# GAT edge values as a row read back from DRAM, and where the softmax of the second layer stands in the round

## The chip, the cores and the metric

The kernel runs on one core of one Trainium2 chip. The core has TensorE for matrix products (PE in the profile; its weight loads are shown as PEld), VectorE (DVE), ScalarE (ACT) and GpSimd (POOL) for everything elementwise, and SyncE (SP), whose queue issues nearly all transfers here. The metric is the time of one execution on the device in microseconds, and the number given is the median of three runs.

## The reference

64 graphs of 256 nodes with 512 features go through two layers. Each layer normalises its input, cuts it at zero, computes a graph operator on it and adds the result to its input.

```
h = max(layernorm(x), 0)
# layer 0: gated attention, 8 heads of 64
q, k, v = h Wq.T, h Wk.T, h Wv.T
c = softmax(q k.T / 8 where adj != 0) v
gate = sigmoid([c, h] Wg.T + bg)
x = x + gate * h + (1 - gate) * c
# layer 1: GAT, one head
h = max(layernorm(x), 0)
Wh = h W
e[i, j] = leaky_relu(Wh[i].a1 + Wh[j].a2, slope 0.2), masked where adj == 0
x = x + elu(softmax(e over j) Wh)
```

All of it is in 32-bit floats. The change concerns layer 1: the values Wh[j].a2 have to stand as a row along the free dimension on all partitions, while the product that makes them leaves them as a column, one value for each node on its partition.

## The kernel before

A graph is two tiles of 128 nodes. The dense products are split into 2 x 2 blocks and done with seven block products in place of eight (Strassen's scheme): `strassen` gives the steps 1 to 7, and the sums between them are named u1, u2, u3 and c00 to c11. u1 and c00 are ACT copies from PSUM, the others are DVE sums of a PSUM bank and an SBUF tile (L185, L187). Three banks a, b and c are shared by all such products; a later step may write into a bank only when the sum that reads it has been done.

The graphs go through a software pipeline. `emit_round(i)` writes out one round by hand, and the order of its calls is the order of instructions on every engine, as the scheduler is told to leave the five engines alone. In round i, graph p = i + 1 is at the q/k and v products, graph i at its attention weights, graph q = i - 1 at the gate, the first residual and the second norm, graph r = i - 2 at Wh, the GAT softmax and its product, and o = i - 3 at the elu, the second residual and the store. On PE a round runs: gate (pma_z to pmc_z), Wh (wh), q/k (qk), v, attention product (pc, L418), scores (ps, L338), GAT product (po, L615).

Transposes over all 128 partitions are mostly done through DRAM: DVE turns 32 x 32 blocks, SP sends the tile to DRAM (`send`, `send_blocks`) and fetches it back with blocks exchanged (`fetch`, `fetch_blocks`). Every such tile is named there_... on its way out: there_e and eT (attention weights; four fetches a round, named by half and pair), there_y and yT (output of the gate), there_h and hT (normalised inputs of both layers), there_g and egT (GAT attention).

SP's queue is in order: a transfer whose semaphores are not there yet holds all that are behind it. The same holds on each engine.

The steps around the change, for graph r, or q where it is said:

- The last column of each half of w1 carries W a1 and W a2, so that Wh holds one more column per half (HH + 1 = 257 columns). The a2 column is `wh[:, t, 1, HH]`.
- `g_edges` (L552 to L556) makes the row of 256 values on all 128 partitions with two PE transposes of the column, broadcast to 128 columns, into a PSUM tile pe.
- `g_logits` (L558 to L564) adds row, own value and mask with one DVE instruction for each of the two tiles; `g_leaky` (L566 to L571) does the leaky relu and the negated maximum; `g_exp` (L578) is ACT; `g_turn_e` (L587 to L598) turns blocks on DVE; `g_send_e` and `g_fetch_e` take the result through DRAM; `g_out` (L611 to L617) needs it as egT.
- For the last three graphs (g >= LAST - 1 = 61) the softmax is transposed on PE in place of DRAM.
- `g_residual` (L502 to L509), for graph q, adds yT to x with one DVE sum per tile; `g_stats` and `g_root` follow.
- `g_elu`, `g_add` (L637, POOL) and `g_store` (L640) end graph o. `load_graph` (L88 to L94) fetches x and adj of graph i + 2 into a pool of five x tiles, so that its x waits for the store of graph o to have landed.
- `a_fetch(i, 1, 1)` is the fourth eT; the second half of pc reads it last.

The pool "tmp" has five buffers of 128 x 512 floats, among them eg and egT; "h" has one, which the normalised inputs and the gate's output y share.

Of the kernel before, what the change touches and what calls it, by code (L numbers as in the profile page):

```python
# [8 lines left out]
F32 = mybir.dt.float32  # L9
# [3 lines left out]
ALU = mybir.AluOpType  # L13
# [9 lines left out]
def kernel(  # L23
# [32 lines left out]
    nc = tc.nc  # L56
    B, N, H = x.shape
    NH = 8
    DK = H // NH
    P = 128  # L60
    HC = H // P
    NT = N // P
    HH = H // 2
    SCALE = 1.0 / DK ** 0.5
    LAST = B - 2
    assert N == 256 and H == 512 and SCALE == 0.125

    def pool(name, bufs, **kw):
        return ctx.enter_context(tc.tile_pool(name=name, bufs=bufs, **kw))
# [3 lines left out]
    sb = {tag: pool(tag, bufs) for tag, bufs in {  # L73
        "x": 5, "adj": 1, "mask": 4, "hT": 3, "S": 3, "qk": 2, "v": 2, "wh": 1, "e": 5,
        "cT": 1, "z": 2, "h": 1, "tmp": 5, "U": 3,
    }.items()}
# [3 lines left out]
    dram = pool("dram", 4, space=bass.MemoryType.DRAM)  # L80
# [6 lines left out]
    graphs = {}  # L87
# [38 lines left out]
    def edge_columns():  # L126

        w = weight["1"]

        def column(c, side):  # L130
            scr = sb["tmp"].tile([P, 2, HH], F32, tag="t", name=f"scr_{c}_{side}")
            nc.vector.scalar_tensor_tensor(
                scr, w[:, c, :, :HH], 1.0, a_sb[side].rearrange("p (n f) -> p n f", n=2),
                ALU.mult, ALU.mult, accum_out=w[:, c, side, HH:],
            )

        return [lambda c=c, side=side: column(c, side) for c in range(HC) for side in range(2)]
# [177 lines left out]
    def on_tokens(w, op):  # L315

        def todo(n):
            return [((), op[n][:, c, :], w[n][:, c, :]) for c in range(2)]
        return todo
# [182 lines left out]
    def g_residual(g, t):  # L502
        s = graphs[g]
        x = s["x"][:, t, :]
        if g >= LAST:
            nc.vector.tensor_tensor(x, x, s["py"][t], ALU.add)
        else:
            x = x.rearrange("p (j i c) -> p j i c", i=4, c=32)
            nc.vector.tensor_tensor(x, x, s["yT"][:, :, t].rearrange("p i j c -> p j i c"), ALU.add)  # L509

    def g_stats(g, t):
        norm_stats(graphs[g], t, f"l1_{g}")
# [33 lines left out]
    def g_wh(g):  # L546
# [2 lines left out]
        dst = [[s["wh"][:, t, n, :] for n in range(2)] for t in range(2)]  # L549
        return strassen(f"wh_{g}", [P, HH + 1], on_tokens(weight["1"], s["h1S"]), dst)  # L550

    def g_edges(g):  # L552
        s = graphs[g]
        pe = s["pe"] = ps["w"].tile([P, N], F32, tag="t", name=f"pe_{g}")
        for t in range(NT):
            nc.tensor.transpose(pe[:, t * P:(t + 1) * P], s["wh"][:, t, 1, HH:].to_broadcast([P, P]), ident)  # L556

    def g_logits(g):  # L558
        s = graphs[g]
        e = s["eg"] = sb["tmp"].tile([P, NT, N], F32, tag="t", name=f"eg_{g}")  # L560
        for t in range(NT):
            nc.vector.scalar_tensor_tensor(
                e[:, t, :], s["pe"], s["wh"][:, t, 0, HH:], s["mask"][:, t, :], ALU.add, ALU.add
            )  # L564

    def g_leaky(g):  # L566
# [79 lines left out]
    def chore(steps, n):  # L646
        for _ in range(min(n, len(steps))):
            steps.pop(0)()

    def emit_round(i):  # L650


        p, q, r, o = i + 1, i - 1, i - 2, i - 3

        def do(fn, g, *args):
            if 0 <= g < B:
                fn(g, *args)

        def run(fn, g, steps):
            if 0 <= g < B:  # L660
                if (fn, g) not in products:
                    products[fn, g] = fn(g), set()
                product, done = products[fn, g]
                for step in steps.split():
                    if step not in done:
                        product(step)
                        done.add(step)
# [52 lines left out]
        do(p_sums, p)  # L720
        do(g_turn, q)
        do(g_send, q)
        do(a_fetch, i, 0, 1)
        run(g_wh, r, "c10 3 c01")
        do(g_fetch, q)
        do(a_fetch, i, 1, 0)

        if i == -1:
            chore(weight_sums("q"), 4)
            chore(weight_sums("k"), 4)  # L730
        run(p_qk, p, "1 u1")
        do(g_edges, r)
        do(g_logits, r)
        do(g_leaky, r)
        run(p_qk, p, "6 u2 5")
        do(g_elu, o, 1)
        do(g_add, o, 1)
        do(g_add, o, 0)
        do(g_store, o)
        do(g_exp, r)  # L740
        do(g_turn_e, r)
        do(g_send_e, r)
        do(g_rec, r)
        run(p_qk, p, "7 u3 c11 2 c00")
        do(load_graph, p + 1)
        if i == -1:
            for key in ("gh", "gc", "1"):
# [3 lines left out]
            chores.append(lambda: nc.vector.tensor_scalar_mul(hbg, hbg, 0.5))  # L751
            chores.extend(edge_columns() + weight_sums("1"))
        chore(chores, 1)
        do(a_fetch, i, 1, 1)
        do(g_fetch_e, r)
        do(g_residual, q, 0)
        run(p_qk, p, "4 c10")
        do(g_residual, q, 1)
        chore(chores, 1)
        run(p_qk, p, "3 c01")  # L760
        chore(chores, 1)
        do(g_stats, q, 0)
        if i == -1:
# [94 lines left out]
```

## Time and profile before

The median of three runs is 3191.97 us (3191.17 to 3193.47). The execution that was profiled took 3185.72 us, 1.8 us more than the span that the profile shows.

| what | value |
|---|---|
| time, median of three | 3191.97 us |
| the profiled execution: time, span | 3185.72 us, 3183.9 us |
| length of a round (1525.81 to 1574.16, pc to pc) | 48.35 us |
| of it busy: PE, DVE, ACT, POOL | 48.35, 38.27, 22.06, 23.52 us |
| share of the DMA engines in that round | 0.80 |
| granted TensorE clock | 0.994 |
| transposes pe on PE (L556) | 128, 274 ns each |
| logits (L562), leaky (L569), maximum (L571) on DVE | 480, 692, 686 ns (middle) |
| first residual on DVE (L509) | 124, 686 ns each |
| second residual on POOL (L637) | 128, 1272 ns each |

Read it in this way. A busy PE is not by itself proof that PE is the limit, so one looks at the chain of waits: the run of work that ended last, followed backwards from the end. Where it stays on one engine without gaps, time falls only if work of that engine falls, and it rises as soon as something else comes too late for it. For an in-order queue the question is which transfer stands behind which wait. Landing times are given from the start of the issue to the last of the data's completion. On the queue, an entry with x4 is four issues in a row.

### The profile page before, as it was taken

How to read it: one execution, taken by the hardware profiler on the slowest of the kernel's cores; microseconds unless marked ns; L12 is line 12 of the kernel's file. 1: busy time of each engine (PE TensorE's matmuls, PEld its weight loads, DVE VectorE, ACT ScalarE, POOL GpSimd, SP SyncE). 2: the span in 40 equal slices, each digit the busy share in tenths (PEclk: the TensorE clock that was granted, in tenths of full speed). 3: DMA queues.
4: the chain of work that ended last, by engine and by line, in shares of the span. 5: the costliest groups of instructions: out<-in, count | busy, mean ns of one | idle time of the engine just before them, and what ended most of it. 6: DMA issues, size and time to landing. Idle time of an engine off the chain costs nothing.

```text
span 3183.9 us, 66670 instructions
## 1 busy us (share of the span) xinstructions
PE 3125.0 (98%) x22716; PEld 2723.9 (86%) x22716; DVE 2467.8 (78%) x6366; ACT 1413.6 (44%) x3976; POOL 1506.3 (47%) x2183
## 2 busy tenths in 40 slices
PE   7899999999999999999999999999999999999997
PEld 6888888888889888888888898888888888888984
DVE  6777877877877878778778778778787787787774
ACT  2343543543544534435435445445344344454442
POOL 2454544544544545535445445445454454454453
PEclk9999999999999999999999999999999999999998
DMA  5678778777777777787787777777877877877761
GB/s 169 176 173 204 189 180 206 185 180 206 182 190 199 184 191 195 180 203 187 178 211 184 181 207 182 190 197 177 200 189 182 205 186 179 211 183 183 204 170 44
DMA packets 1103394, 590.63 MB, mean 186 GB/s; under 512 B 685776, under 2 KB 1029328, under 8 KB 1103056
## 3 DMA queue, kind: packets, MB, share of 16 engines
q1 hardware_dynamic: 1102000, 585.32, 73.9%
q8 instruction: 182, 2.98, 0.4%
q14 instruction: 156, 1.28, 0.1%
q10 hardware_dynamic: 1056, 1.05, 0.1%
HBM read 304.88 MB, written 281.28 MB: 184 GB/s over the span
## 4 chain that ended last, share of the span: by engine, by line
PE 90%; DVE 4%; POOL 2%; DMA 2%; issue 1%; SPq 1%; ACT 0%; DVEq 0%; POOLq 0%; ACTq 0%
PE pmb_qk L174 11%; PE pmb_z L174 9%; PE pc L418 7%; PE pma_qk L174 7%; PE pmc_qk L174 7%; PE ps L338 6%; PE po L615 6%; PE pma_z L174 6%; PE pmc_z L174 6%; PE pmb_v L174 5%; PE pmb_wh L174 5%; PE pma_v L174 3%; PE pmc_v L174 3%; PE pmc_wh L174 3%; PE pma_wh L174 3%; DVE e L353 1%
## 5 line engine op out<-in xcount | busy, mean ns | idle before, releaser
L362 ACT ACTIVATE e<-e,low 128x256 f32<-128x256 f32 x1024 | 506.5, 499 | 63.3 <-DVE low L353 63.3
L204 POOL TENSOR_TENSOR rs_l<-ve_l,mhalf 128x2 f32<-128x2 f32 x128 | 89.0, 695 | 869.7 <-DVE ve_l L200 869.7
L353 DVE CUSTOM_DVE_ANT_0 e<-ps,mask 128x256 f32<-128x256 f32 x1024 | 362.1, 415 | 100.1 <-PE ps L338 100.1
L377 POOL TENSOR_SCALAR e<-e,rec 128x256 f32<-128x256 f32 x768 | 352.7, 477 | 148.8 <-DVE rec L370 100.4
L386 DVE STREAM_TRANSPOSE eb<-e 128x512 f32<-128x512 f32 x512 | 351.8, 696 | 76.7 <-POOL e L377 63.4
L213 ACT ACTIVATE h_l<-x,nb_l,rs_l 128x512 f32<-128x512 f32 x256 | 194.1, 805 | 212.4 <-DVE nb_l L208 123.5
L152 POOL TENSOR_TENSOR S_l<-hT_l 128x256 f32<-128x256 f32 x128 | 93.4, 730 | 395.9 <-DMA hT_l<-there_h 361.9
L637 POOL TENSOR_TENSOR x<-x,pos 128x512 f32<-128x512 f32 x128 | 160.1, 1272 | 229.3 <-DVE pos L633 229.3
L615 PE MATMUL po<-wh,egT 128*128 128x512 f32 x512 | 242.5, 617 | 2.1 <-ACT egT L598 2.1
L338 PE MATMUL ps<-qk 64*128 64x256 f32 x2048 | 238.9, 383 | 0.6 <-DVE v L185 0.6
L418 PE MATMUL pc<-eT,v 128*64 128x256 f32 x2048 | 235.9, 382 | 0.1
L338 PEld LDWEIGHTS ps<-qk 64*128 64x128 f32 x2048 | 193.1, 187 | 45.3 <-DVE ve_l L200 21.9
L418 PEld LDWEIGHTS pc<-eT,v 128*64 128x64 f32 x2048 | 141.3, 137 | 86.7 <-DMA eT<-there_e 16.3
L239 DVE STREAM_TRANSPOSE h_l<-h_l 128x512 f32<-128x512 f32 x248 | 167.8, 695 | 54.7 <-ACT h_l L213 54.7
L615 PEld LDWEIGHTS po<-wh,egT 128*128 128x128 f32 x512 | 94.3, 194 | 118.5 <-issue 95.1
L362 ACT ACTIVATION_READ_ACCUMULATOR e<-e,low 128x1 f32 x1024 | 194.8, 190 | 0.0
L196 DVE BATCH_NORM_STATS2 bs_l<-x 128x6 f32<-128x512 f32 x256 | 172.9, 675 | 5.4 <-DMA x<-in_x_dram 5.4
L461 ACT ACTIVATE z<-z,hbg 128x256 f32<-128x256 f32 x256 | 116.1, 502 | 105.9 <-DVE z L185 105.9
L456 POOL TENSOR_TENSOR d<-hT_l,cT 128x512 f32<-128x512 f32 x128 | 160.5, 1274 | 0.0
L428 ACT COPY cT<-pc 128x512 f32<-128x512 f32 x128 | 74.9, 585 | 184.5 <-PE pc L418 184.5
L174 PEld LDWEIGHTS pma_z<-hT_l,wgh_sb 128*128 128x128 f32 x1024 | 129.2, 192 | 30.4 <-issue 30.4
L174 PE MATMUL pma_qk<-hT_l,wq_sb 128*128 128x128 f32 x1024 | 139.6, 280 | 11.9 <-DMA hT_l<-there_h 10.1
(146 smaller groups left out, 7964.8 us busy)
## 6 DMA issues: line engine op xcount, KB each, us to landing
there_e<-eb SPq DMA_DIRECT2D x256, 512.0 KB, 3.4
eT<-there_e SPq DMA_DIRECT2D x1024, 128.0 KB, 3.9
there_h<-h_l SPq DMA_DIRECT2D x496, 128.0 KB, 3.3
hT_l<-there_h SPq DMA_DIRECT2D x496, 128.0 KB, 3.3
x<-in_x_dram SPq DMA_DIRECT2D x64, 512.0 KB, 4.0
out_dram<-x SPq DMA_DIRECT2D x64, 512.0 KB, 4.2
there_y<-y SPq DMA_DIRECT2D x62, 512.0 KB, 3.3
yT<-there_y SPq DMA_DIRECT2D x248, 128.0 KB, 3.4
```

Of the source, the lines that this page charges most:

```text
L174: nc.tensor.matmul(bank[key][(slice(None), *cols)], lhsT, rhs, start=first and i == 0, stop=last and i == len(todo) - 1, skip_group_check= ...
L196: nc.vector.bn_stats(bs, s["x"][:, t, :])
L213: nc.scalar.activation(h[:, t, :], s["x"][:, t, :], AF.Relu, bias=s["nb"][:, t:t + 1], scale=s["rs"][:, t:t + 1])
L239: nc.vector.transpose(h[:, t, :], h[:, t, :])
L338: nc.tensor.matmul(psc[jj, i][:, t, :], qk[r:r + DK, 0, jj, t * P:(t + 1) * P], qk[r:r + DK, 1, jj, :], start=True, stop=True,)
L353: nc.vector.tensor_tensor_reduce(s["e", half, jj][:, i, t, :], s["ps", half][jj, i][:, t, :], s["mask"][:, t, :], -SCALE, HUGE, ALU.add, A ...
L362: nc.scalar.activation(e, e, AF.Exp, bias=s["low", half][:, jj, i, t:t + 1], scale=-1.0, accum_out=s["sums", half][:, jj, i, t:t + 1],)
L377: nc.gpsimd.tensor_scalar(e, e, rec[:, i, t:t + 1], 1.0, ALU.mult, ALU.mult)
L386: nc.vector.transpose(s["eb", half, jj][:, :, 4 * i:4 * i + 4, :].rearrange("p b n c -> p n b c"), e)
L418: nc.tensor.matmul(pc[i * DK:(i + 1) * DK, jj, :].rearrange("p (t a c) -> p t a c", t=NT, c=32), s["v"][:, kc, hd * DK:(hd + 1) * DK], eT[ ...
L456: nc.gpsimd.tensor_tensor(d, s["hT"][:, :, js, :], s["cT"][:, :, js, :], ALU.subtract)
L615: nc.tensor.matmul(pm, s["egT"][:, t, kc, :], s["wh"][:, kc, :, :HH], start=(kc == 0), stop=(kc == NT - 1))
```

## The change

Three things change.

First, for graphs below 61 the row of a2 values is made without PE. `g_send_edges` writes the column of 256 values from Wh to DRAM (one transfer, elements of four bytes), and `g_fetch_edges` reads those 1,024 bytes back onto each of the 128 partitions, straight into the first half of eg. `g_logits` then reads the row from eg, so it does tile 1 first and tile 0 in place.

Second, the order of the round changes. On SP the two transfers stand around the eT fetch (0, 1), ahead of the yT fetch; the eT fetch (1, 0) goes behind the store; the load of x and adj goes ahead of there_g; the fourth eT fetch stays behind there_g. On DVE the logits, leaky and maximum move from behind the first step of the q/k product to behind u3 and c11; the block transpose of the softmax moves behind c10.

Third, the first residual of graphs below 62 moves from DVE to POOL; its second sum is issued behind the last step of the q/k product.

```diff
             x = x.rearrange("p (j i c) -> p j i c", i=4, c=32)
-            nc.vector.tensor_tensor(x, x, s["yT"][:, :, t].rearrange("p i j c -> p j i c"), ALU.add)
+            nc.gpsimd.tensor_tensor(x, x, s["yT"][:, :, t].rearrange("p i j c -> p j i c"), ALU.add)
...
+    def g_send_edges(g):
+        s = graphs[g]
+        if g < LAST - 1:
+            s["edges"] = dram.tile([NT, P], F32, tag="edges", name=f"edges_{g}")
+            with nc.allow_non_contiguous_dma(reason="a column of 256"):
+                nc.sync.dma_start(s["edges"].rearrange("t p -> p t"), s["wh"][:, :, 1, HH])
+
+    def g_fetch_edges(g):
+        s = graphs[g]
+        if g < LAST - 1:
+            s["eg"] = sb["tmp"].tile([P, NT, N], F32, tag="t", name=f"eg_{g}")
+            row = s.pop("edges").rearrange("t p -> (t p)")
+            nc.sync.dma_start(s["eg"][:, 0, :], bass.AP(tensor=row.tensor, offset=row.offset, ap=[[0, P], [1, N]]))
+
     def g_edges(g):
         s = graphs[g]
+        if g < LAST - 1:
+            return
...
     def g_logits(g):
         s = graphs[g]
-        e = s["eg"] = sb["tmp"].tile([P, NT, N], F32, tag="t", name=f"eg_{g}")
-        for t in range(NT):
+        if g >= LAST - 1:
+            s["eg"] = sb["tmp"].tile([P, NT, N], F32, tag="t", name=f"eg_{g}")
+        e = s["eg"]
+        for t in (1, 0):
             nc.vector.scalar_tensor_tensor(
-                e[:, t, :], s["pe"], s["wh"][:, t, 0, HH:], s["mask"][:, t, :], ALU.add, ALU.add
+                e[:, t, :], s["pe"] if g >= LAST - 1 else e[:, 0, :], s["wh"][:, t, 0, HH:], s["mask"][:, t, :], ALU.add, ALU.add
             )
...
         do(g_send, q)
+        run(g_wh, r, "c10 3 c01")
+        do(g_send_edges, r)
         do(a_fetch, i, 0, 1)
-        run(g_wh, r, "c10 3 c01")
+        do(g_fetch_edges, r)
         do(g_fetch, q)
-        do(a_fetch, i, 1, 0)
...
         run(p_qk, p, "1 u1")
-        do(g_edges, r)
-        do(g_logits, r)
-        do(g_leaky, r)
         run(p_qk, p, "6 u2 5")
         do(g_elu, o, 1)
         do(g_add, o, 1)
         do(g_add, o, 0)
         do(g_store, o)
+        do(a_fetch, i, 1, 0)
+        run(p_qk, p, "7 u3 c11")
+        do(g_edges, r)
+        do(g_logits, r)
+        do(g_leaky, r)
+        run(p_qk, p, "2 c00")
         do(g_exp, r)
-        do(g_turn_e, r)
-        do(g_send_e, r)
-        do(g_rec, r)
-        run(p_qk, p, "7 u3 c11 2 c00")
         do(load_graph, p + 1)
...
+        run(p_qk, p, "4 c10")
+        do(g_turn_e, r)
+        do(g_send_e, r)
         do(a_fetch, i, 1, 1)
+        do(g_rec, r)
+        do(g_residual, q, 0)
         do(g_fetch_e, r)
-        do(g_residual, q, 0)
-        run(p_qk, p, "4 c10")
-        do(g_residual, q, 1)
         chore(chores, 1)
         run(p_qk, p, "3 c01")
+        do(g_residual, q, 1)
```

## The prediction

> **What bounds the kernel now.** I read four views in this order: the page's busy shares and chain, the chain of waits of one round in order of time, the time line of the queues and of VectorE (DVE) and GpSimd (POOL) in that round, and the landing times of single transfers.
>
> ```profile
> PE 3125.0 (98%) x22716; PEld 2723.9 (86%) x22716; DVE 2467.8 (78%) x6366; ACT 1413.6 (44%) x3976; POOL 1506.3 (47%) x2183
> PE 90%; DVE 4%; POOL 2%; DMA 2%; issue 1%; SPq 1%; ACT 0%; DVEq 0%; POOLq 0%; ACTq 0%
> ```
>
> TensorE (PE) is busy for 98% of the span and makes 90% of the chain that ends last; nothing else has 5%. So only two things count: PE work removed, and PE made to wait. One round, from the chain:
>
> ```profile
> 1507.12 1.78 PE pma_qk L174 x16
> 1508.90 0.22 PE pe L556 x2
> 1509.12 1.79 PE pmb_qk L174 x16
> ...
> 1514.48 1.79 PE pma_qk L174 x16
> 1516.26 1.79 PE pmb_qk L174 x16
> ...
> 1525.88 3.61 PE pc L418 x32
> ```
>
> The two transposes take 0.22 us of PE, once a round. The attention product pc follows 16.76 us later without a gap. Step 7 of the q/k product ends at 1514.48, step 4 at 1518.05. Now the queue and the tightest transfer:
>
> ```profile
> 1515.37 0.40 SPq L640 DMA_DIRECT2D out_dram<-x x1
> 1516.00 3.00 SPq L248 DMA_DIRECT2D there_g<-eg x4
> 1519.93 0.40 SPq L92 DMA_DIRECT2D x<-in_x_dram x1
> 1520.37 0.47 SPq L93 DMA_DIRECT2D adj<-in_adj_dram x1
> 1520.89 1.89 SPq L397 DMA_DIRECT2D eT<-there_e x4
> ...
> 1522.87 3.23 SPq L255 DMA_DIRECT2D egT<-there_g x4
> ```
>
> ```profile
> L397 SPq DMA_DIRECT2D eT<-there_e x4: 430/432/465, 1520.9 to 1522.3; - x4
> DMA to landing us min/median/max: 5.1/5.4/5.8
> ```
>
> This fourth eT is used by the last quarter of pc, whose weights load about 2.4 us after pc starts (24 of 32 loads; 1525.8 + 2.4 = 1528.2). It lands at 1522.3 + 5.8 = 1528.1: 0.1 us to spare here. The next two rounds spare about 0.9 us (issued to 1570.7, landing in 5.0, pc from 1574.2). A round earlier it lands at 1479.9 (issued to 1474.2, landing in 5.7), and pc takes 3.98 us on the time line in place of 3.6. So PE already touches this transfer.
>
> ```profile
> 1493.73 1.19 DVE L633 SCALAR_TENSOR_TENSOR pos<-neg,pos 128x512 f32<-128x512 f32 x1
> 1494.33 1.18 POOL L154 TENSOR_TENSOR S_l<-hT_l 128x256 f32<-128x256 f32 x1
> 1512.08 0.68 DVE L633 SCALAR_TENSOR_TENSOR pos<-neg,pos 128x512 f32<-128x512 f32 x1
> ```
>
> The same DVE instruction takes 0.68 us alone and 1.19 us beside a POOL sum, and the POOL sum 1.18 in place of 0.73: the two wait for one another.
>
> [...] The trace has 3.5 us for a quiet eT fetch (issued 1503.7 to 1505.2, landing in 3.5/3.5/3.6). [...] here 1.27 us (L637) against 0.69 (L509).
>
> **The change part by part.** I keep the clock of the round whose pc starts at 1525.8, so what stands before the removed transposes shifts 0.22 us later.
>
> Removed: 2 transposes in 61 graphs (g < 61; the last three keep them): 61 x 0.22 = 13.4 us of PE. From DVE two sums of 0.69 a round, worth nothing by themselves, since DVE is not on the chain.
>
> The row through DRAM. wh is complete at 1508.02 + 0.22 = 1508.2. The column of 256 4-byte values is issued then, behind there_y (512 KB, issued at 1507.6, which lands in 3.0 in this trace). Bounds of its landing: 2.4 us (a little under there_g's median 3.0 to 3.7, for 64 KB) to 6 us (small writes dear); I take 2.9, just behind there_y: 1511.1. eT (0,1) is issued meanwhile, to 1511.0. The row fetch then lands 3.5 later, at 1514.7, in time for the logits at 1515.9. Nothing of this is on PE, but the queue stands until the column has landed, and yT follows: issued 1511.6 to 1512.9.
>
> Logits and softmax. DVE takes u3 at 1514.5, c11 at 1515.2, two logits 1515.9 to 1516.7 (0.41 each, [...] 0.48 from PSUM before), leaky 0.69 and maximum 0.69 to 1518.1 (L569, L571), ACT the two exponentials 1.1 to 1519.2, DVE the transpose 0.71 to 1520.0. Before, it ended at 1513.4.
>
> The queue. The sum L633 comes about 0.7 earlier, so the store goes at 1514.8 and x, adj at about 1519.1 to 1520.0 (x waits for the store's landing, 4.2 to 4.5). there_g now stands behind them and waits for the transpose: 1520.0 to 1523.0. The fourth eT stands behind there_g: issued 1523.1 to 1524.6, landing in 3.5 because the loads ahead of it have drained: 1528.1, against 1528.2 needed. This is the central number: **the slack of the softmax chain is nil**. Bounds: 3.5 (quiet) to 4.3 (the window's median for eT): a stall of 0 to 0.7; I take 0.1. egT then goes at 1526 to 1528.6 and lands by 1532.2, 0.9 before po. The h1 blocks leave 1.7 us later (1528.6) and land at 1533.8, which holds the next ACT norm by up to 1 us; ACT has 0.6 us before pos and DVE 0.7 before the reciprocal to hide it, and beyond that the loss is small.
>
> Residual on POOL. yT lands 3.0 to 3.7 after its last issue (1512.9): about 1516.3. POOL is free from 1514.9 on (two L637 sums), so it starts two sums of 1.27 at 1516.4. At that time DVE is in the second logit and about to do leaky. In their new form both have two SBUF inputs (eg and mask; eg and eg), where the logits read PSUM before. A residual that begins before leaky holds it for up to 1.27; one before the second logit can hold it and then leaky, 2.5 in all; one that begins after leaky has started (1516.7) costs nothing, as maximum, transpose and sums from PSUM have one SBUF input. Queued on DVE behind leaky: maximum, c10, the transpose, c01, statistics and u2 of v, for whose bank PE's step 7 waits. All this delay reaches there_g and eT, and PE in full, as there is no slack. My yT stands 0.3 before leaky with a spread of about 0.5 (landings of one kind spread so), so some seven rounds in ten collide, at 1.0 to 2.4, say 1.3: 0.9 a round.
>
> Sum: a round gains 0.22 and loses 0.1 + 0.9 = 1.0: 61 x 0.78 = 47.6 us. The profiled execution took 3185.7 us (span 3183.9); 3185.7 + 47.6 = 3233.3. The median shown, 3191.97, is 6.3 above that execution, so the forecast is 3240.
>
> **The rivals.**
> 1. Faster: no collision. If the column takes 3.3 us or more, yT lands behind the start of leaky and POOL's sums run beside one-input work. Then 0.05 is lost and 61 x 0.17 = 10 us won: 3182. It decides from 0.4 us more on the column, and ends at about 4.1, where the row itself misses the logits. For it: a 4-byte write may well be slow. Against: there_y, 512 KB, lands in 3.0.
> 2. A draw: the stall of eT is 0.12 to 0.32 (landing in 3.7 to 3.9) without collisions: 3186 to 3198. For it: 3.9 is the page's median for eT.
> 3. Slow small writes: the column lands in 6 us, the row at 1517.8, the logits 1.9 late; PE waits 2.0: 61 x 1.78 = 109 us: 3300. Against: the 512 biases of 4 B, loaded at the start, land in 8.3, like the full rows ahead of them (8.1 to 8.6); but those are reads of DRAM, not writes.
> That the change does less than it says is out: in the order of instructions 61 graphs lose their transposes.
>
> **How the numbers follow.** Forecast 0.53, at 3205 to 3300 by collisions in three to all rounds of ten at up to 2; faster 0.30; draw 0.09; slow writes 0.08. A change of 0.2% (6.4 us) is what can be told from none. Slower by more: 0.53 + 0.08 = 0.61; same 0.09, faster 0.30. The range must reach the faster case, so 3176 to 3300; the forecast's own is 3205 to 3300.
>
> **What would show it.** In the changed trace: no pe but in the last three graphs; DVE's leaky or second logit stretched from 0.69 or 0.41 to 1 us and more beside POOL's residual; eT's last issue at or behind 1 us before pc; PE idle inside pc (3.6 becomes 4.6) or before step 7 of v. If leaky stays at 0.69 in nearly all rounds and pc at 3.6 to 3.7, rival 1 or 2 holds and I am wrong; if the logits wait for the row, rival 3.

## The result, and the profile after

| | before | after |
|---|---|---|
| time, median | 3192.49 us (3191.17 to 3193.47) | 3640.33 us (3634.86 to 3644.33) |
| ratio | 1 | 1.140, 95% interval 1.139 to 1.142 |
| span of the profiled execution | 3183.9 us | 3638.3 us |
| length of a round (mean of rounds 3 to 61, pc to pc) | 48.47 us | 55.92 us |
| mean granted TensorE clock | 0.994 | 0.944 |

The kernel became 14% slower: 448 us. The forecast was 3240, the range 3176 to 3300. The sign was right, the size was wrong by a factor of nine. The page of the changed kernel, its busy shares and its chain:

```profile
PE 3276.2 (90%) x22594; PEld 2796.5 (77%) x22594; DVE 2381.0 (65%) x6242; ACT 1408.2 (39%) x3976; POOL 1661.8 (46%) x2307
...
PE 45%; DMA 25%; DVE 17%; POOL 6%; issue 3%; SPq 3%; ACT 1%; DVEq 0%; POOLq 0%; ACTq 0%
```

PE held 90% of the chain before and holds 45% now; a quarter is DMA. PE also became busier, by 151.2 us (3276.2 less 3125.0), though the transposes are gone. PE's idle time (span less busy) grew from 58.9 to 362.1 us, so the whole loss is there: 303.2 + 151.2 = 454.4 us of span. These are two questions: what does PE wait for, and why are its matmuls slower? The chain of waits of one round of the changed kernel (start, length, what):

```profile
1717.56 0.66 DVE wh L185 x2
...
1718.23 10.62 DMA edges<-wh
...
1728.93 3.74 DMA eg<-edges
...
1732.69 0.50 DVE eg L581
...
1735.14 0.61 DVE qk L185
...
1735.80 2.07 PE pmb_v L174 x4
```

Read it from above: wh is complete, the column of 256 values goes out, and 10.62 us later the row may be fetched. That takes 3.74. Only then can DVE form the logits, and the sum of step c10 (`qk L185`), which is queued behind logits, leaky and maximum, frees the bank that PE's v product needs. The waits of the changed kernel (who waited for what, us in all, times, longest) show the same steps in all rounds:

```profile
POOL x L509 <- DMA yT<-there_y: 624.4, 62, 14.3
DVE eg L581 <- DMA eg<-edges: 398.7, 61, 8.7
...
PE pmb_v L174 <- DVE qk L185: 297.0, 61, 7.0
```

PE's 297.0 us are nearly all of its new idle time of 303.2. The largest wait, 624.4 us of POOL for yT, does not stand in the chain of the round shown. SyncE's queue in the same round (start, length of issuing):

```profile
1717.59 0.34 SPq L392 DMA_DIRECT2D there_y<-y  x1
1718.23 0.38 SPq L558 DMA_DIRECT2D edges<-wh  x1
1718.70 2.01 SPq L397 DMA_DIRECT2D eT<-there_e  x4
1728.93 0.34 SPq L565 DMA_DIRECT2D eg<-edges  x1
1729.44 2.35 SPq L397 DMA_DIRECT2D yT<-there_y  x4
1731.89 0.40 SPq L659 DMA_DIRECT2D out_dram<-x  x1
```

Between 1720.7 and 1728.9, for 8.2 us, the queue issues nothing: it stands at the row's fetch, and yT, the store and all that follows stand behind it. Over the whole run this is SyncE's largest wait:

```profile
SPq L565 <- DMA edges<-wh: 418.5, 60, 8.5
```

The second question is answered by the table by stage of the changed kernel: busy time of each engine in four stretches, then the granted clock of PE (the column with 1.00, 0.77, 0.50, 1.00) and the share of the DMA engines.

```profile
1724.00:1730.00 6.00, 6.00 (x54) 5.97 (x54) 1.38 (x2) 0.58 (x1) 0.83 (x1) 1.00 0.58 20
1730.00:1735.80 5.80, 0.67 (x5) 0.25 (x3) 2.95 (x5) 0.62 (x3) 0.03 (x1) 0.77 0.98 208
1735.80:1740.00 4.20, 4.20 (x10) 3.02 (x11) 3.40 (x9) 0.72 (x3) 2.59 (x3) 0.50 0.91 245
1740.00:1745.00 5.00, 5.00 (x32) 3.82 (x32) 3.24 (x8) 1.77 (x3) 0.58 (x1) 1.00 0.89 210
```

The columns are length, PE, PEld, DVE, ACT, POOL, clock, DMA share and GB/s, so the clock reads 1.00, then 0.77 while PE stands, then **0.50 for the 4.2 us after the wait**, then 1.00. By the clock alone these 4.2 us hold what takes 2.1 us at 1.00 (an estimate from the column); four matmuls of pmc_v take 1.91 us in the chain of this round and 0.86 in that of before. The groups of the v product, before and after (busy us, mean ns of one, idle before):

```profile
L174 PE MATMUL pmb_v<-wv_t,S_l 128*128 128x256 f32 x512 | 131.5, 379 | 1.9 <-DVE wv_t L110 1.9
L174 PE MATMUL pmc_v<-wv_sb,S_l 128*128 128x256 f32 x512 | 131.4, 379 | 0.0
L174 PE MATMUL pma_v<-wv_sb,hT_l 128*128 128x256 f32 x512 | 131.6, 379 | 0.0
```

```profile
L174 PE MATMUL pmb_v<-wv_t,S_l 128*128 128x256 f32 x512 | 214.2, 562 | 298.9 <-DVE qk L185 297.0 <-DVE wv_t L110 1.9
L174 PE MATMUL pmc_v<-wv_sb,S_l 128*128 128x256 f32 x512 | 191.5, 511 | 5.3 <-DVE qk L185 5.3
L174 PE MATMUL pma_v<-wv_sb,hT_l 128*128 128x256 f32 x512 | 139.8, 398 | 0.0
```

The same instructions are longer by 82.7 us (pmb_v), 60.1 (pmc_v) and 8.2 (pma_v): 151.0 us together, and it is the step behind the wait that grows most. With the steps that overlap counted once, the v product keeps PE busy for 161 us longer (548 in place of 387, worked out from the records); the missing transposes take 13 off, all else adds 3, and that is the 151.2. So a round loses 4.97 us to the wait (303.2 / 61) and another 2.6 to the clock after it (161 / 61).

### The profile page after: what moved, and what is told of

It is laid out like the page before. It is cut to its first block, busy times and chain, and to the rows that moved or that the text cites. A ratio compares the mean times of both kernels' runs of the same rounds, so it can differ in the third digit from the quotient of the medians.

```text
span 3638.3 us, 66969 instructions
## 1 busy us (share of the span) xinstructions
PE 3276.2 (90%) x22594; PEld 2796.5 (77%) x22594; DVE 2381.0 (65%) x6242; ACT 1408.2 (39%) x3976; POOL 1661.8 (46%) x2307
## 4 chain that ended last, share of the span: by engine, by line
PE 45%; DMA 25%; DVE 17%; POOL 6%; issue 3%; SPq 3%; ACT 1%; DVEq 0%; POOLq 0%; ACTq 0%
DMA edges<-wh 12%; DMA eg<-edges 6%; PE pmb_v L174 6%; PE pc L418 5%; PE pmb_z L174 5%; PE ps L338 4%; PE pmc_v L174 4%; PE po L634 4%; POOL e L377 3%; DMA hT_l<-there_h 3%; PE pma_z L174 3%; PE pmc_z L174 3%; DVE e L353 3%; PE pmb_qk L174 2%; PE pmb_wh L174 2%
## 5 line engine op out<-in xcount | busy, mean ns | idle before, releaser
L174 PE MATMUL pmb_v<-wv_t,S_l 128*128 128x256 f32 x512 | 214.2, 562 | 298.9 <-DVE qk L185 297.0
L509 POOL TENSOR_TENSOR x<-x,yT 128x512 f32<-128x512 f32 x124 | 154.7, 1269 | 624.4 <-DMA yT<-there_y 624.4
L174 PEld LDWEIGHTS pmb_v<-wv_t,S_l 128*128 128x128 f32 x512 | 139.2, 286 | 351.0 <-DVE qk L185 321.5
L386 DVE STREAM_TRANSPOSE eb<-e 128x512 f32<-128x512 f32 x512 | 351.6, 696 | 65.6 <-POOL e L377 52.7
L581 DVE SCALAR_TENSOR_TENSOR eg<-eg,wh,mask 128x256 f32<-128x256 f32 x122 | 59.1, 485 | 400.9 <-DMA eg<-edges 398.7
L185 DVE TENSOR_TENSOR u_qk<-pmb_qk,u_qk 128x512 f32<-128x512 f32 x128 | 88.5, 692 | 326.5 <-PE pmb_qk L174 326.4
L597 ACT ACTIVATE eg<-eg,nm 128x256 f32<-128x256 f32 x128 | 64.0, 500 | 509.0 <-DVE nm L590 458.7
L187 ACT COPY qk<-pma_qk 128x512 f32<-128x512 f32 x64 | 37.4, 585 | 426.4 <-PE pma_qk L174 380.5
L174 PE MATMUL pmc_v<-wv_sb,S_l 128*128 128x256 f32 x512 | 191.5, 511 | 5.3 <-DVE qk L185 5.3
```

Of the source, the lines that this page charges most:

```text
L174: nc.tensor.matmul(bank[key][(slice(None), *cols)], lhsT, rhs, start=first and i == 0, stop=last and i == len(todo) - 1, skip_group_check= ...
L386: nc.vector.transpose(s["eb", half, jj][:, :, 4 * i:4 * i + 4, :].rearrange("p b n c -> p n b c"), e)
L509: nc.gpsimd.tensor_tensor(x, x, s["yT"][:, :, t].rearrange("p i j c -> p j i c"), ALU.add)
```

## The experiments

The theory: a write of the column in 256 pieces of four bytes takes about 10 us, and this alone makes the loss. The rivals: the row's read or its place in the queue; the residual on POOL; the new order. 14 kernels were run.

### The column left out, and the column turned first

The first fetches the row from an input that is there from the start (the column is not written, and the logits are formed from other values). The second keeps the computation: DVE copies the column over 128 x 32 and turns it in 32 x 32 blocks, so that eight runs of 128 bytes are written.

```diff
-                nc.sync.dma_start(s["edges"].rearrange("t p -> p t"), s["wh"][:, :, 1, HH])
...
-            nc.sync.dma_start(s["eg"][:, 0, :], bass.AP(tensor=row.tensor, offset=row.offset, ap=[[0, P], [1, N]]))
+            nc.sync.dma_start(s["eg"][:, 0, :], bass.AP(tensor=a.tensor, offset=a.offset, ap=[[0, P], [1, N]]))
```

> Leaves out: the column of a2 values is not written to DRAM; the row that is read back onto all partitions is 256 values of the input a, so the GAT logits are wrong by that row. All else is the changed kernel. Theory C (the 4-byte column write lands in some 10.7 us, and the logits, which stand ahead of c10 on DVE, hold PE for 7 us a round): 3175 to 3250 us, the row in time, PE no longer waiting for DVE at the first use of bank b by v. Rival O (the new order, or the residual on GpSimd, costs most of it): still above 3500 us. Rival P (anything small at this place of the queue lands late): the row read would be late too, above 3400 us.

```diff
+            s["eg"] = sb["tmp"].tile([P, NT, N], F32, tag="t", name=f"eg_{g}")
+            c = s["eg"][:, 1, 0:32]
+            nc.vector.tensor_copy(c.rearrange("p (t k) -> p t k", t=NT), s["wh"][:, :, 1, HH:].to_broadcast([P, NT, 16]))
+            nc.vector.transpose(c, c)
...
-                nc.sync.dma_start(s["edges"].rearrange("t p -> p t"), s["wh"][:, :, 1, HH])
+            nc.sync.dma_start(s["edges"].rearrange("t (k f) -> k t f", f=32), c[0:128:16, :])
```

> The column is turned on DVE first (a broadcast copy to 128x32 and one 32x32 block transpose, two small instructions), so that the write to DRAM is 8 runs of 128 B in place of 256 of 4 B, at the same place of the queue. Theory C: the write lands in 2.4 to 3.5 us, time 3175 to 3250 us. Inside this span, my forecast's step on the residual (GpSimd's sums collide with leaky on DVE) says 3205 to 3250, its rival 3175 to 3190. Rival P: the write lands in 10 us as before, time 3600 us and more. Rival O: above 3500 us.

Measured: 3202.55 us without the column (ratio to before 1.003, 1.002 to 1.004), 3205.9 with the turned column (1.0042, 1.0026 to 1.0058). So 434 of the 448 us are the form in which the column is written (3640.3 less 3205.9): the row, its fetch on 128 partitions, the order and POOL's residual are all still there. The turned column lands in 1.6 us (median of 61, worked out from the completion records). The transfers of `edges` in the kernel with the turned column (its write, the fetch of the row, who waited for them, and the row's landing):

```profile
L561 SPq DMA_DIRECT2D edges<-eg x61: 570/573/642, 151.5 to 3076.3; - x61
L567 SPq DMA_DIRECT2D eg<-edges x61: 349/360/371, 154.5 to 3080.0; - x61
...
  DVE eg L583: 11.0, 18
...
DMA to landing us min/median/max: 3.1/4.0/5.0
```

DVE's wait for the row is 11.0 us where it was 398.7. A little is left that the change does not earn: 13 us above before (0.42%), though 13 us of transposes are gone. The chain of this kernel at the end of a round shows where:

```profile
1728.73 2.74 PE pc L418 x24
1731.47 0.09 issue
1731.56 1.08 PE pc L418 x8
```

The last eight matmuls of pc, those of the fourth eT, stand apart from the others. In the mean of rounds 3 to 61, pc takes 3.68 us from its first to its last start in place of 3.31, and the v product 6.37 in place of 6.14.

### What makes the column slow: columns in other layouts

The kernel before gets one more DMA a round, which nothing reads: the same column, in four layouts by turns, then in four more. It stands behind wh, ahead of the eT fetch (0, 1).

```diff
+    def g_column(g):
+        col = graphs[g]["wh"][:, :, 1, HH]
+        kind = "abcd"[g % 4]
+        far = {"a": 1, "b": 16, "c": 128, "d": 1}[kind]
+        there = dram.tile([NT, P, far], F32, tag=f"col{kind}", name=f"col{kind}_{g}")
+        there = there[:, :, 0].rearrange("t p -> p t")
...
+            if kind == "d":
+                nc.sync.dma_start(there[:, 0:1], col[:, 0:1])
+            else:
+                nc.sync.dma_start(there, col)
```

> The kernel before, to which one more transfer is added that nobody reads: the a2 column is written to DRAM at the place where the changed kernel does it, in four layouts by graph: a, 256 values in a row of 1 KB; b, 256 values 64 B apart; c, 256 values 512 B apart; d, 128 values in a row. Theory C1 (writes of 4 B that fall into the same few lines of DRAM wait for one another): a lands in 10 to 11 us, d in 5.5 to 7, b and c in 3 to 5. Theory C2 (every 4-byte write is dear wherever it goes): a, b and c in 10 to 11, d in 5.5 to 7. Rival P: all four alike. Time 3190 to 3230 us, more if the queue stands for the completion of the late write.

The second run has `far = {"a": 2, "b": 4, "c": 8, "d": 32}` and always the whole column.

> The kernel before with one added DMA a round, which nothing reads: the column of 256 values is written to DRAM with its values 8 bytes apart (every fourth graph), 16, 32 or 128 bytes apart, so 8, 4, 2 values or 1 in a line of 64 bytes. If writes into one line wait for one another, the landing falls with the number that share it: about 6 us at 8 bytes, 4 to 5 at 16, 3 to 4 at 32, 3 at 128. If it is only that adjacent values are in one transfer or one row of memory, all four land alike, near 3 or near 10 us.

Median time from the issue to the last completion that the trace holds, 16 columns of each kind, worked out from the completion records:

```
values apart   values in 64 bytes   landing, us (5% to 95%)
  4 bytes            16             10.2  (9.0 to 11.6)    first run, a
  4 bytes            16              9.3  (7.5 to 10.8)    first run, d: 128 values only
  8 bytes             8              5.0  (4.2 to 5.8)     second run, a
 16 bytes             4              3.7  (2.9 to 4.5)     second run, b
 32 bytes             2              3.3  (2.1 to 4.1)     second run, c
 64 bytes             1              3.0  (2.1 to 3.9)     first run, b
128 bytes             1              3.0  (2.1 to 4.0)     second run, d
512 bytes             1              3.1  (2.3 to 4.2)     first run, c
the changed kernel's own: 61 columns 9.6  (8.8 to 11.0)
```

The size of a write is four bytes in every row of the table, and the count is 256 in all but one. What the time follows is how many values lie close together. At 64 bytes apart the price is gone, and at 32 what is left of it is within the spread of single columns (3.3 against 3.0). Half as many values, as close together, cost nearly the same, which I had expected at 5.5 to 7: so the price is hardly one of the count. The transfer of the second run with values 8 bytes apart (durations of its issue in ns, then its landing):

```profile
L559 SPq DMA_DIRECT2D cola<-wh x16: 382/382/1036, 151.4 to 3102.6; - x16
...
DMA to landing us min/median/max: 4.2/5.0/6.0
```

The first run took 3422.3 us (a single run; before 3194.3), far more than the 3190 to 3230 expected, though nothing reads these columns. Its queue shows one way in which they cost (SyncE's waits):

```profile
SPq L397 <- DMA there_y<-y: 102.3, 27, 8.7
...
SPq L397 <- DMA cola<-wh: 46.0, 8, 6.9
...
SPq L397 <- DMA cold<-wh: 19.4, 5, 6.3
```

The fetches on the same queue wait for the columns, and for there_y, which was issued **ahead** of them. They wait for a column that they don't read because of the semaphores: in the records of the trace before each transfer reports its landing on one of eight semaphores, taken in turn, and in all 3,269 cases in which one is used again its last transfer had landed. The yT fetch that waits here is the eighth transfer after the column. there_y itself is late as well: in this run it lands in 6.0 us (median) ahead of columns of the first kind and 8.4 ahead of the fourth, but in 3.3 and 3.5 ahead of the second and third. In the changed kernel it lands in 7.6 us in place of 3.3 before. So the transfer in front of a slow write lands late with it; by what way was not shown. The second run took 3231.4 us (a single run; before 3192.9).

### One part of the change at a time

```diff
-            nc.vector.tensor_tensor(x, x, s["yT"][:, :, t].rearrange("p i j c -> p j i c"), ALU.add)
+            nc.gpsimd.tensor_tensor(x, x, s["yT"][:, :, t].rearrange("p i j c -> p j i c"), ALU.add)
```

This line alone, in the kernel before:

> The kernel before with the first residual moved from DVE to GpSimd, nothing else. Theory S (what is left of the loss once the column lands early, 11 us in e2_turned, comes from the fourth eT standing behind there_g and from the late row): the residual alone is neutral, 3188 to 3200 us. Rival R (the residual on GpSimd costs, [...]through its 1.27 us): above 3204 us.

Measured: 3191.83 us, ratio 1.0002 (0.9993 to 1.0010). Moving the residual is worth nothing there. The order of the changed kernel and the residual on POOL, with the row made by two transposes on PE as before (the two new transfers are left out of the queue):

```diff
     def g_edges(g):
         s = graphs[g]
-        if g < LAST - 1:
-            return
...
-        do(g_send_edges, r)
...
-        do(g_fetch_edges, r)
```

> The changed kernel's order and its residual on GpSimd, but the row made by the two transposes on PE for all graphs, just ahead of the logits; no column and no row through DRAM. Theory S: the stall at the fourth eT stays, 0.3 to 0.4 us a round, the transposes cost their 0.22 again, and the wait for the row is gone: 3204 to 3225 us, slower than before. Rival D (the way through DRAM costs what is left, the order is free): 3188 to 3197 us.

Measured: 3206.79 us, ratio 1.0047 (1.0032 to 1.0061), the same as with the turned column (3205.9). So the order and the residual on POOL together cost 15 us, and a row through DRAM, quickly written, gives nothing in place of two transposes: PE's 0.22 us a round are saved and lost again at pc (3.68 us in place of 3.36 here).

Where the 15 us go is seen in leaky on DVE, the instruction that the prediction expected to be held up. All its durations (min, median, max in ns) in this kernel, then in the one without the column:

```profile
L586 DVE SCALAR_TENSOR_TENSOR eg<-eg x64: 691/1361/1809, 160.2 to 3183.8; 128x512 f32<-128x512 f32 x64
```

```profile
L585 DVE SCALAR_TENSOR_TENSOR eg<-eg x64: 691/692/1802, 161.4 to 3179.9; 128x512 f32<-128x512 f32 x64
```

In this kernel leaky is stretched in 51 of the 59 rounds 3 to 61, each time beside a sum of the first residual on POOL. Where it takes up to 1.2 us the v product takes 6.14 us, as before (21 rounds); beyond that v grows with it, in most rounds one for one, to 6.73 us at the longest leaky. Summed up this is 13 of the 15 us. Without the column it is 13 of 59 rounds, with v at 7.17 us in these and 6.16 in the other 46. With the turned column leaky is never held up by the first residual. There v takes 6.14 in 36 rounds and grows in the others with DVE's wait for the row, to 7.89 where that is 1.8 us. (All of this paragraph is worked out from the records.) So two kernels with the same time lose it in different ways. This rests on the rounds of single traces: the new order with the transposes and with the residual on DVE was not run.

The line of the residual undone in the changed kernel, and in the kernel with the turned column:

> The changed kernel with the residual back on DVE. Theory C: 3625 to 3660 us, as the residual waits for the late yT in either place. Rival O in the form that the residual on GpSimd costs: below 3400 us.

> The kernel with the turned column, with the residual on VectorE as in the kernel before. With the column late, putting it back there cost 111 us, for VectorE then waited itself for yT. Theory: with yT on time the place of the residual is worth next to nothing, as in the kernel before: within 0.3% of 3206. Rival: VectorE's two adds of about 0.4 us a round stand ahead of work that TensorE waits for, and it is 10 to 25 us slower than 3206.

Measured: 3751.22 us with the slow column (one run), 111 more and not the same as the changed kernel; 3248.29 with the turned one (ratio 1.0171, 1.0157 to 1.0185), 42 more. Both expectations of no effect missed. In the first, DVE itself now stands where POOL stood, for a yT that is late, and what it holds up is the chain (all waits of that kernel; these are its third and seventh lines):

```profile
DVE eg L581 <- DMA eg<-edges: 452.5, 61, 9.3
...
PE pmb_v L174 <- DVE qk L185: 349.4, 61, 7.6
```

PE waits 349.4 us for the sum c10, where it waited 297.0. In the second, PE's waits are these:

```profile
PE pmb_v L174 <- DVE u_v L185: 37.2, 61, 0.6
PE pmc_v L174 <- DVE qk L185: 12.5, 21, 1.4
```

Two sums of 0.69 us on DVE stand ahead of the sum u_v, and PE waits for that in each of 61 rounds. In the order of before the residual's place is worth nothing; in the new order, where the softmax and c10 come just ahead of the v product, POOL's help is worth 42 us, though it brings the collisions shown above where yT is early. It was no side matter of the change but what made its order bearable.

### Can the new order be mended?

All six start from the kernel with the turned column. Each moves one or two lines.

The fourth eT fetch goes behind the third:

```diff
         do(a_fetch, i, 1, 0)
+        do(a_fetch, i, 1, 1)
         run(p_qk, p, "7 u3 c11")
...
         do(g_send_e, r)
-        do(a_fetch, i, 1, 1)
```

> e2_turned with the fourth eT fetch issued right behind the third, ahead of the loads and of there_g. Theory S: the stall inside pc (0.37 us a round in e2_turned) goes, and what is left is the late row and a few collisions (0.23 a round before v ends): 3178 to 3192 us. Rival R or D: 3200 us or more, as the eT fetch was not what cost.

As that, and the fetch of the row goes ahead of the second eT:

```diff
-        do(a_fetch, i, 0, 1)
         do(g_fetch_edges, r)
+        do(a_fetch, i, 0, 1)
```

> e8_eT_ahead with the row fetched right behind its column, ahead of the second eT fetch, so that it lands some 2 us earlier while yT keeps its place. Theory S: the logits no longer wait for the row; 3170 to 3184 us, the 13.4 us of the transposes won in full or nearly so. Rival: the same time as e8_eT_ahead within 3 us, when the row was not what delayed v.

The fourth eT fetch goes to ScalarE's queue, behind u1:

```diff
-        fetch(eT.rearrange("p a n c -> p a (n c)"), s.pop(("there", half, jj)))
+        fetch(eT.rearrange("p a n c -> p a (n c)"), s.pop(("there", half, jj)), nc.scalar if half and jj else nc.sync)
...
         run(p_qk, p, "1 u1")
+        do(a_fetch, i, 1, 1)
...
         do(g_send_e, r)
-        do(a_fetch, i, 1, 1)
```

> The kernel with the turned column (3205.9 us, a round of 48.75) with one edit: the fourth of the four eT fetches is issued on ScalarE's queue, right behind the sum u1 of q and k, where it stood late on SP's queue before. Theory: in that kernel TensorE stands 0.37 us a round at pc's last matmuls for that fetch; issued early it lands early, and since SP's other transfers keep their places, nothing that reads them moves. Expected 3180 to 3195, pc's wait below 0.1 us a round. Rival: the quarter's send lands too late for it, so ScalarE stands at the issue of the DMA and what is queued behind it (the copies c11 and c00, and the exponential) comes later: over 3200, with a wait of the ScalarE queue for the DMA of the send.

That with the row ahead of the second eT, by the same edit as above:

> As the run with the fourth eT fetch on ScalarE's queue, and the fetch of the row is issued ahead of the second eT fetch, right behind the column. Theory: the row then lands 0.5 to 1 us earlier, DVE's logits no longer wait for it, and the v step that needs the bank of c10 begins 0.1 to 0.2 us a round earlier: 6 to 12 us below that run. Rival: the eT fetch that goes behind the row is now the later one, and TensorE's pc waits for it: no faster than that run.

The load of the next x and adj goes behind the fourth eT:

```diff
-        do(load_graph, p + 1)
...
         do(a_fetch, i, 1, 1)
+        if i != -1:
+            do(load_graph, p + 1)
```

> The kernel with the turned column (3205.9 us), with the load of the next x and adj moved behind the fourth eT fetch (from the first round on). Theory: there_g and the fourth eT go 0.5 us earlier (there_g at the end of the softmax's transpose, 1723.0 in place of 1723.5 in the round shown), the wait at pc falls from 0.24 to below 0.05 us a round: 3188 to 3197. Rival: the late transpose alone sets it, or x and adj, which now land 4 us later, are late for the norms behind them: 3203 or more.

Or between there_g and the fourth eT:

```diff
         do(g_send_e, r)
+        if i != -1:
+            do(load_graph, p + 1)
         do(a_fetch, i, 1, 1)
```

> As the run with the load behind the fourth eT, but the load goes between there_g and the fourth eT, as in the kernel before. Theory: the fetch is as late as in the kernel with the turned column, since the same transfers stand ahead of it; only there_g is earlier: 3200 to 3208. Rival: what counts is there_g, which egT and the fetch's neighbours wait for: as fast as the run with the load behind.

None is faster than the kernel with the turned column. The gain expected of the first two did not come, nor the draw expected of the last; for ScalarE's queue and for the load behind the rival came, the former by another way than it said; with the row first on ScalarE's kernel the time fell by 7.5 us, where 6 to 12 were expected (the two intervals just overlap), but another wait had taken over. The table has PE's idle time by the tile that it waited to begin, in us a round (means of rounds 3 to 61, worked out from the records; waits within a matmul's modelled end don't count).

```
kernel                        time, us  ratio (95%)              round   PE idle a round before
before                        3192      1                        48.47   pma_qk 0.07
order, row by transposes      3206.79   1.0047 (1.0032, 1.0061)  48.75   pma_qk 0.09, pc 0.04
turned column                 3205.90   1.0042 (1.0026, 1.0058)  48.75   pc 0.24, pmc_v 0.06
  fourth eT ahead             3243.23   1.0162 (1.0147, 1.0177)  49.45   pmb_z 0.75, po 0.07, pma_qk 0.07
  and row first               3284.38   1.0291 (1.0275, 1.0306)  50.02   pmb_z 1.02, po 0.34
  fourth eT on ScalarE        3301.22   1.0336 (1.0321, 1.0350)  50.27   pmc_v 0.70, pmb_v 0.53
  and row first               3293.69   1.0303 (1.0283, 1.0323)  50.24   pmb_v 1.06, pmb_z 0.34
  load behind                 3237.40   1.0126 (1.0111, 1.0141)  49.27   ps 0.19, pc 0.12
  load between                3401.78   1.0643 (1.0613, 1.0673)  52.15   pc 2.67
```

The edits took away or halved the wait they were aimed at (the last one aside), and another took its place:

- Fourth eT ahead: pc no longer waits, but the blocks of h1 are sent later, and the one buffer of "h" holds ACT's next norm (first line below, from the waits of that kernel), so what stands behind it on ACT and DVE, u_z among it, is late for PE. With the row first both waits grow (ACT's to 215.3 us, PE's to 62.6).

```profile
ACT h_l L213 <- DMA there_h<-h_l: 144.5, 39, 4.9
...
PE pmb_z L174 <- DVE u_z L185: 44.5, 51, 2.0
```

- Fourth eT on ScalarE: the row comes late, by the semaphores again. With the four fetches of the second queue taking their turn, the row's fetch comes to a semaphore that a fetch of the second eT took only 3.5 us earlier (with the turned column alone it was last taken 6.9 us earlier), and waits until that fetch has landed. It waits so in every round, and with the turned column alone in none. The row itself lands in 4.5 us in place of 4.0. The waits of SyncE and of DVE in that kernel:

```profile
SPq L567 <- DMA eT<-there_e: 77.2, 61, 2.0
```

```profile
DVE eg L583 <- DMA eg<-edges: 122.7, 61, 3.3
```

- That with the row first: now the row is in time (0.7 us in all), but yT is issued later, and through POOL's residual and the statistics that is what PE waits for. The waits of that kernel:

```profile
POOL x L509 <- DMA yT<-there_y: 384.5, 62, 13.3
...
DVE bs_l L196 <- POOL x L509: 87.7, 61, 3.2
...
PE pmb_v L174 <- DVE u_v L185: 68.2, 61, 3.4
```

- Load behind: x comes too late for its statistics; the line is from the transfers of x in that kernel.

```profile
  DVE bs_l L196: 180.8, 61
```

- Load between: the fourth eT now stands behind the load's two large transfers (512 and 256 KB). The chain of waits of that kernel:

```profile
1722.39 5.73 DMA eT<-there_e
1728.17 1.97 PE pc L418 x8
```

The fetch lands in 5.73 us, and PE waits 2.67 us a round in the mean. Here too the clock pays, as the table by stage of that kernel has it (the columns as above):

```profile
1726.00:1728.20 2.20, 0.03 (x2) 0.03 (x2) 0.04 (x1) 0.00 (x0) 2.00 (x3) 0.76 1.08 192
1728.20:1732.00 3.80, 3.80 (x18) 2.32 (x20) 0.00 (x0) 0.58 (x1) 2.52 (x5) 0.50 0.84 127
```

After a wait of some 3 us (0.9 of it ahead of the first line: PE is busy for 3.08 of the 4 us before 1726.0) the clock is 0.50 over the next 3.8 us. So it is the place of the load ahead of there_g that keeps the fourth eT nearly in time, and the expectation that it would make no difference was wrong by 190 us.

No kernel that was tried beats the one before. A column 64 bytes apart with a row read from it was not tried: the read would then be in pieces of four bytes. Nor was the row through DRAM in the order of before.

## Why the prediction was wrong

**What bounds the kernel; the path: right.** The prediction said that two things count, PE work removed and PE made to wait, and that the queue stands until the column has landed, with yT behind it. Both are in the trace after: 418.5 us of SyncE waiting at the row's fetch, and PE's 297.0.

**The step that failed is the landing of the column**: "Bounds of its landing: 2.4 us ... to 6 us (small writes dear); I take 2.9". It is 9.6 us in the median and 10.62 in the round shown, outside of both bounds. The nearest row that I used, there_g, is a write of 64 KB in runs of many bytes; no row of the trace had writes of four bytes side by side, and the upper end was an estimate of mine, set by nothing but a doubling. Size alone isn't the price: 256 writes of four bytes, each by itself in 64, land in 3.0 us. The bound should have been left open, and the third rival given far more than 0.08.

**The third rival had the mechanism and one term too few.** Its sum, with 9.6 in place of 6: PE waits 2.0 + 3.6 = 5.6, and 61 x (5.6 - 0.22) = 328 us: 3520. The wait measured is 4.87 (297.0 / 61), 45 us less; that the sum c10 still had some room before the v product is the likely reason, which no run isolates. What is missing is the clock: 161 us in the v product, as above. 3520 - 45 + 161 = 3636, against 3640. In the round shown, 5.1 us of idle are followed by 4.2 us at 0.50. Over the whole run (worked out from the records) each of the 60 waits of 3.5 us and more was followed by work at 0.50, for 4.7 us in the mean, which costs half of that, 2.3. Shorter waits show no sharp limit: with the load between, 25 of 53 waits of 2.0 to 3.5 us were followed by 0.50 and the others weren't. No wait of this size was in the forecast, so I hadn't priced it. By these runs, whoever costs a PE wait of 3.5 us or more should add about 2 to 2.5 for the clock, and for one of 2 to 3.5 us allow for it.

**The row's fetch: nearly right.** 3.5 was taken; 3.74 in the round shown, 4.0 in the median with the turned column. Each of the two logits takes 485 ns with the row in SBUF (L581, median in the changed kernel), where 0.41 was taken.

**"The slack of the softmax chain is nil": right in kind.** A stall of 0.1 at pc was taken, with bounds of 0 to 0.7. With the column quick it is 0.37 (3.68 less 3.31). In the changed kernel itself it doesn't show (3.39), since PE comes late to pc. Beside it the v product loses 0.23 (6.37 less 6.14), there by a row that is late in some rounds. The prediction had the row in time, at 1514.7 for 1515.9, 1.2 us ahead.

**Collisions of POOL's residual with leaky: the mechanism right, how often wrong.** Seven rounds in ten were to collide, at 1.3 us each. With the turned column, the kernel whose column lands early as the forecast had it, none does. All durations of leaky there:

```profile
L590 DVE SCALAR_TENSOR_TENSOR eg<-eg x64: 691/691/1053, 160.1 to 3182.9; 128x512 f32<-128x512 f32 x64
```

The 1053 ns belong to the last three graphs and stand beside the second residual. The first residual begins 1.2 us behind the start of leaky in the mean: the two added instructions on DVE (0.6 us) and the issue of the second eT (2.2 us in the median, up to 3.6) put yT later than I had it. How far a sum of POOL beside it lengthens a DVE instruction can be measured in the trace before (worked out from the records; beside means for 0.1 us or more). L633 on DVE, with both inputs in SBUF, takes 681 ns in the median without a two-input sum of POOL beside it (65 times) and 1192 with one (63 times). In 59 of these it ends 545 to 552 ns after a POOL sum has ended, and the next POOL sum ends 583 to 591 ns after it. Three DVE instructions with one input in SBUF don't show this: the block transpose L386 takes 711 ns without and 695 beside such a sum, the sum u_v (L185, with a PSUM bank) 425 and 425; in the changed kernel the maximum (L590) takes 686 and 686. Leaky is lengthened where yT goes out earlier: with the row by transposes leaky takes up to 1809 ns beside the first residual, 1118 more than the 691 alone. There it is stretched by 0.63 us a round in the mean, but only 0.22 of that reaches v, so "PE in full, as there is no slack" doesn't hold in that kernel. Without the column, the 13 rounds with a collision take 49.62 us and the others 48.38, and 1.24 is close to the 1.3 taken. That the kernel with the turned column is slower than before all the same, by 13 us, was luck for the forecast's direction: it comes from pc and the late row, and not from the collisions that carried the forecast.

**The first rival (no collision, faster by 10) and the draw: did not come.** Collisions stayed away in the kernel with the turned column, and no gain came, because 0.37 us at pc and 0.23 by the late row weigh more than 0.22 of PE work and 0.06 less of idle before the q/k product. There is something in the rival all the same: without the column, where the row hardly ever comes late, those 48.38 us of the 46 rounds without a collision are 0.09 less than before.

**The residual on POOL** was treated as a cost alone (1.27 us a sum there, 0.69 on DVE). By itself it is neutral (1.0002), and in the new order it saves 42 us with the turned column.

## What to carry to other kernels

Before a value per partition is sent to DRAM as a contiguous row, turn it on chip or spread it: 256 writes of four bytes side by side landed in about 10 us and 64 bytes apart in 3.0; eight runs of 128 bytes landed in 1.6, did the same job and cost the kernel 434 us less. When an operation has no row of its kind in the trace, let its upper bound be set by what it would have to cost to decide the case, and price a wait of PE with the clock that it loses afterwards (2.3 us here for each wait of 3.5 us and more). Two kernels of the same time need not lose it in the same place, so a cost is best looked for round by round and not in the mean. In a queue that is full to 0.1 us, a transfer moved ahead moves another one behind: five of six reorderings removed or halved the wait they aimed at, and all six lost more elsewhere.

## What the runs showed of the hardware that was not expected

- Four-byte writes to DRAM from 128 partitions: 10.2 us when 16 lie in 64 bytes, 5.0 with 8, 3.7 with 4, 3.3 with 2, 3.0 with one, and no less at 128 or 512 bytes. That writes into the same 64 bytes wait for one another is a reading that fits (the same 32 fits nearly as well); it was not shown.
- The transfer that was issued 0.6 us ahead of such a column (in the round shown) often completes late as well: there_y in 7.6 us (median) in place of 3.3, and in 37 of 62 rounds later than 5.1, which it never was before.
- A wait of 5.1 us of PE was followed by 4.2 us at a clock of 0.50. In the profiled executions waits of up to 1.4 us a round in the mean (the reordered kernels) left the mean clock at 0.991 to 0.993; the load between, with 2.67 a round in the mean, brought it to 0.975. The shortest wait that was followed by 0.50 there was one of 2.0 us, the longest that was not one of 3.4.
